# The last block's row maxima: two single products a step behind the scores of the same heads, in three banks

## The chip, the cores and the metric

The kernel runs on one core of one Trainium2 chip. The metric is device time in microseconds (us), the median of several runs. In the traces PE is TensorE's matmul side and PEld its weight loads, DVE is VectorE, ACT ScalarE, POOL GpSimd, and SP the engine whose queue issues most of the transfers. L262 means line 262 of the kernel before.

## The reference

Two layers run over a graph of N = 3327 nodes with 128 features, each followed by a residual sum and a layer norm. `adj` is a dense 0/1 matrix with ones on its diagonal.

```python
# layer 0
cos = beta[0] * (x @ x.T) / (norm2 @ norm2.T + 1e-07)
P = softmax(cos + (1.0 - adj) * -1e9, axis=1)
x = layernorm(x + P @ x)
# layer 1: d = 128 features, h = 8 heads
q = (x @ Wq.T).reshape(d, n, h)         # k and v alike
a = einsum('dnh,dmh->dnm', q, k) * d ** -0.5
a = softmax(a + adj + adj, axis=2)      # 128 matrices of 3327 x 3327
out = einsum('dnm,dmh->dnh', a, v)
x = layernorm(x + out.reshape(n, h * d) @ Wo.T)
```

Layer 1 is 128 independent attentions ("heads" below), each over 3327 queries and 3327 keys, with a contraction over only 8 numbers. The `reshape` is a plain one, so the heads are cut from the flat row order. Nearly all the time is spent there.

## The kernel before

**Precision.** Queries and keys are split into a high and a low part, so that a contraction over 8 becomes one over 4 x 8 = 32 rows of PE's array. Four heads fill the array's 128 rows, one in each row group of 32, and products of different row groups can be under way at the same time.

**Units and steps.** The 26 tiles of 128 queries are cut into nine blocks: eight of 384 queries and a last one of 256. The heads are cut into 32 groups of four. A unit is one block with one group; there are 288, block by block, and each has 26 steps, one for every tile of 128 keys: 7488 steps. The last block's 32 units are the final 832.

**One step** (loop at L873) makes the exponentials of one key tile for four heads, and multiplies the values by those of two steps ago:

- PE writes for two heads (`hs_b`) the shift, minus the row's maximum, into the two banks of `eb` (`shifts`, L788, matmul on L791) and adds the scores (`scores`, L797).
- ACT takes both through one exponential into `pb` (L898). POOL multiplies by `eT`, the exponential of twice the adjacency (L899).
- PE does the same for the other two heads (`hs_a`) in two banks `ea`, and adds the adjacency there by a product (`add_adj`, L778). ACT takes each bank through an exponential into `pa` (L922). The pool of `ea` has two buffers and a step uses both; `eb` has one of two banks.
- PE multiplies the values by the `pa` and `pb` of two steps ago (`weigh`, L808, `LAG = 2`).

Shifts, scores and search products use row groups of 32; adjacency and values use all 128 rows and groups of columns.

**The search.** The shift needs every row's maximum over all keys, so each score is computed twice: once with queries as output rows for the maximum, 33 steps ahead (`k = s + T + AHEAD`), and once with keys as output rows for the exponential. A search product is 128 queries by 512 keys of one head (L262). A "pair" is two heads' products in the two banks of tile `m2`, reduced by one VectorE instruction (L277); a "single" is one head's product in the one bank `m1`, with a reduction of its own (L298). The rest of the key range, chunk 6 with 256 keys, is done for two query tiles at once (L288, L302). `max_steps` (L231) lists a pair and a single for each of the 52 steps of two units. In a 384-query block each step has one of each. In the last block, two query tiles, a step needs two heads' products on average: even steps have a pair (heads 2, 3) and a single (head 0), odd steps a single (head 1) alone.

**Place in a step.** What is listed in `first` goes between the shifts and the scores of `hs_b`, `late` between the shifts and the scores of `hs_a`. For a 384-query block's search, the pair is first and the single late. For the last block's search, the single is first and the pair late, `hs_b` is always (2, 3) and `hs_a` (0, 1).

**Order.** The order on PE, ACT, DVE and POOL is the order in which the program is written (`manual_schedule`); the framework adds the semaphore waits from the tiles that are read and written. SP's transfers are issued in order too: a unit's keys, queries and values are loaded from step 2 of two units before. After a unit's search is complete, `shift_parts` (L313) makes its shifts ready with one VectorE and four POOL instructions, and in the unit before its own, `shift_turn` (L761) turns them at steps 22 and 23 of a 256-query unit into free columns of `ea`, from where ACT copies them (L916).

Of the kernel before, what the change touches and what calls it, by code (L numbers as in the profile page):

```python
# [10 lines left out]
F32 = mybir.dt.float32  # L11
# [8 lines left out]
P = 128  # L20
# [25 lines left out]
def gnn_two_layers(  # L46
# [116 lines left out]
    QB = QT * P  # L163
# [8 lines left out]
    units = [(b, g) for b in range(NB) for g in range(G4)]  # L172
# [4 lines left out]
    def width(b):  # L177
        return min(QT, T - b * QT) * P
# [46 lines left out]
    class Banks:  # L225
        pair = single = None
# [4 lines left out]
    def max_steps(u, w):  # L231

        if width(units[u][0]) == 2 * P:
            full = [((q,), c) for q in range(2) for c in range(6)] + [((0, 1), 6)]
            pairs = [x for v in (u, w) for k in full for x in ((v, (2, 3), *k), None)]
            ones = [(v, (a,), *k) for v in (u, w) for k in full for a in range(2)]  # L240
            return list(zip(pairs, ones))
        full = [((q,), c) for q in range(3) for c in range(6)]
        left = ((0, 1), 6)

        def one(v, hs, ks):
            return [(v, (a,), *k) for k in ks for a in hs]

        lo, hi = (0, 1), (2, 3)
        pairs = [(u, lo, *k) for k in full[:12]] + [(u, hi, *k) for k in full[:13]]
        pairs += [(u, hi, (2,), 6), (u, lo, (2,), 6)]  # L250
        last = one(w, hi, full[12:] + [left])
        ones = one(u, hi, full[13:] + [left]) + one(u, lo, full[12:] + [left]) + last[:1]
        pairs += [(w, hi, *k) for k in full[:12]]
        pairs += [(w, lo, *k) for k in full[:13]]
        ones += one(w, lo, full[13:] + [left]) + last[1:]
        assert len(pairs) == len(ones) == 2 * T
        assert not any(set(p[1]) & set(x[1]) for p, x in zip(pairs, ones))
        return list(zip(pairs, ones))
# [50 lines left out]
    def search(step):  # L309
        if step is not None:  # L310
            (max_pair if len(step[1]) == 2 else max_single)(*step)
# [32 lines left out]
    with ExitStack() as l0:  # L344
# [222 lines left out]
        with tc.manual_schedule(  # L567
# [9 lines left out]
            w = (T - 1) * P  # L577
# [7 lines left out]
            ones = const.tile([P, P], F32, name="ones")  # L585
# [30 lines left out]
            for c in range(NCH):  # L616
                tp, a, b = turn(ps_tp, lambda t: xn[:, t, :], c)
# [90 lines left out]
    with ExitStack() as at:  # L708
# [3 lines left out]
        ps_m = at.enter_context(tc.tile_pool(name="at_m", bufs=1, space=PSUM))  # L712
# [118 lines left out]
        with tc.manual_schedule(  # L831
            engines={
                mybir.EngineType.PE,
                mybir.EngineType.Activation,
                mybir.EngineType.DVE,
                mybir.EngineType.Pool,
            }
        ):
            for j in range(T):
                load_adj_tile(0, j)  # L840
            for i in range(2):
                load_values(us[i])
            us[0].kx = own.tile([P, NP], F32R, name="kx", bufs=2)
            nc.gpsimd.tensor_copy(
                us[0].kx.rearrange("p (t k) -> p t k", t=T),
                us[0].km.bitcast(F32).rearrange("p (k t) -> p t k", t=T),
            )
            keep_keys(us[0])
            for k in range(k_first, T + AHEAD):
                first_max(k)  # L850
            for j in range(T):
                exp_adj_tile(0, j)

            pp = at.enter_context(tc.tile_pool(name="at_p", bufs=4))
            ps_a = at.enter_context(tc.tile_pool(name="at_a", bufs=2, space=PSUM))
            ps_b = at.enter_context(tc.tile_pool(name="at_b", bufs=1, space=PSUM))
            ps_o = at.enter_context(tc.tile_pool(name="at_o", bufs=1, space=PSUM))
            acc = ps_o.tile([P, 512], F32, name="acc")
            nc.vector.memset(acc, 0.0)
            one = fix.tile([P, P], BF16, name="one")  # L860
            nc.vector.tensor_copy(one, ones)

            def new_a():
                return [ps_a.tile([P, 512], F32, name="ea") for _ in range(2)]

            e = ps_b.tile([P, 2, 512], F32, name="eb")
            for q in range(QT):
                shift_turn(us[0], q, e[:, 0, q * P : (q + 1) * P], True)
            nc.scalar.copy(us[0].cx, e[:, 0, :QB])  # L869

            todo = []
            turn = []
            for s in range(NU * T + LAG):  # L873
                i, j = divmod(s, T)
                u = us.get(i)
                if u is not None:
                    if j == 2 and i + 2 < NU:
                        load_keys(new_unit(i + 2))
                        load_queries(us[i + 2], own.tile([P, QB], F32R, name="qx"))
                        load_values(us[i + 2])  # L880
                    if j == 12 and i + 4 < G4:
                        gather(i + 4)
                    k = s + T + AHEAD
                    pair, single = max_step(k) or (None, None)

                    full = pair is not None and width(units[pair[0]][0]) == QB
                    first = pair if full else single
                    late = single if full else pair
                    hs_a = pair[1] if full else (0, 1)
                    hs_b = tuple(h for h in range(4) if h not in hs_a)  # L890

                    e_b = ps_b.tile([P, 2, 512], F32, name="eb")
                    b01 = [e_b[:, x] for x in range(2)]
                    shifts(u, b01, hs_b)
                    search(first)
                    scores(u, j, b01, hs_b, True)
                    pt_b = pp.tile([P, 2, QB], F32, name="pb")
                    nc.scalar.activation(pt_b[:, :, : u.nq], e_b[:, :, : u.nq], AF.Exp)  # L898
                    nc.gpsimd.tensor_tensor(  # L899
                        pt_b[:, :, : u.nq],  # L900
                        pt_b[:, :, : u.nq],
                        eT[:, j, : u.nq].unsqueeze(1).to_broadcast([P, 2, u.nq]),
                        ALU.mult,
                    )
                    e_a = new_a()
                    shifts(u, e_a, hs_a)
                    search(late)
                    scores(u, j, e_a, hs_a, False)
                    free = e_a[0][:, QB:]
                    x = us.get(i + 1)  # L910
                    copies = []
                    q = j - (T - 4)
                    if x is not None and 0 <= q < x.nt:
                        shift_turn(x, q, free, False)
                        copies.append(
                            lambda: nc.scalar.copy(x.cx[:, q * P : (q + 1) * P], free)  # L916
                        )
                    pt_a = pp.tile([P, 2, QB], F32, name="pa")
                    for h, e in enumerate(e_a):
                        add_adj(e, u, j)  # L920
                    for h, e in enumerate(e_a):
                        nc.scalar.activation(pt_a[:, h, : u.nq], e[:, : u.nq], AF.Exp)  # L922
                    for f in copies:
                        f()
                    if x is not None and not x.b:
                        order_keys(x, j)
                        if j == T - 1:
                            keep_keys(x)
                    pts = {}
                    for x in range(2):  # L930
                        pts[hs_a[x]], pts[hs_b[x]] = pt_a[:, x], pt_b[:, x]
                    todo.append((u, j, pts))

                    if k % (2 * T) in (T, 2 * T - 1):
                        v = us.get(k // (2 * T) * 2 + (k % (2 * T) > T))
                        if v is not None:
                            shift_parts(v)
                if s >= LAG:
                    w = todo.pop(0)
                    weigh(*w)  # L940
                    if w[1] == T - 1:
                        take(us.pop(w[0].i))

                if turn and turn[0][0] <= s:
                    exp_adj_tile(*turn.pop(0)[1:])
                if u is not None and i + 1 < NU and units[i + 1][0] != u.b:
                    load_adj_tile(u.b + 1, j)
                    turn.append((s + 5, u.b + 1, j))


    with ExitStack() as fi:
# [49 lines left out]
        w = (T - 1) * P  # L1001
# [43 lines left out]
```

## Time and profile before

The median of three runs is 15358.9 us (15358.85 to 15360.56).

| | |
|---|---|
| profiled execution | 15361.32 us, span 15359.5 us |
| mean granted TensorE clock | 0.995 |
| PE busy | 15192.6 us, 99% |
| DVE, POOL, ACT busy | 13818.7 (90%), 13765.0 (90%), 12755.2 us (83%) |
| DMA | 66 GB/s on average |
| search products (L262) | 23128 of 512 columns, 6804.0 us on PE, 471 ns each |
| pair reductions (L277) | 6753, 1225 ns each |
| single reductions (L298) | 6371, 681 ns each |

The busy time of one engine overlaps that of the others. Matmuls are pipelined, and their ends are modelled, so rows of PE overlap each other as well: the sum of their durations is far more than the span. The means of the groups above mix the blocks of 384 and of 256 queries. The last block's search runs from about 13923 us, while the eighth block's last steps are still under way, to about 15211 us.

### The profile page before, as it was taken

The page shows a single profiled execution, that of the slowest core. Times are in us where ns is not written, and L with a number is a line of the kernel's source. Part 1 is how long each engine was busy: PE and PEld are TensorE (multiplying, and loading weights), DVE is VectorE, ACT ScalarE, POOL GpSimd, SP SyncE. Part 2 cuts the span into 40 slices and gives each one's busy share as a digit, 9 for nine tenths or more (in the row PEclk, how much of TensorE's full clock was granted, in tenths as well). Part 3 has the DMA queues.
Part 4 walks back from the last instruction along what each step waited for, and adds up shares of the span by engine and source line. Part 5 has one row for each costly group of instructions (what it writes and reads, how often), then busy time and mean ns, then how long its engine had stood idle before and what let it go on. Part 6 is the DMA issues. An engine that isn't in the chain of part 4 may idle for free.

```text
span 15359.5 us, 494776 instructions
## 1 busy us (share of the span) xinstructions
PE 15192.6 (99%) x210460; PEld 6695.5 (44%) x210460; DVE 13818.7 (90%) x15851; ACT 12755.2 (83%) x25413; POOL 13765.0 (90%) x8979
## 2 busy tenths in 40 slices
PE   8899999999999999999999999999999999999999
PEld 5534444444444444444444444444444444444555
DVE  7889999999999999999999999999999999998776
ACT  7689998888888888888888888888888888888777
POOL 3389999999999999999999999999999999998887
PEclk9999999999999999999999999999999999999999
DMA  7732221111111111111111111111111111111112
GB/s 229 226 103 97 101 98 60 48 51 48 56 50 47 52 53 53 46 53 46 60 47 53 47 58 48 51 48 55 51 46 53 46 59 46 53 46 62 62 59 83
DMA packets 553135, 1018.81 MB, mean 66 GB/s; under 512 B 148711, under 2 KB 493284, under 8 KB 504582
## 3 DMA queue, kind: packets, MB, share of 16 engines
q1 hardware_dynamic: 547126, 965.00, 19.1%
q0 software_dynamic: 3792, 22.15, 0.8%
q8 instruction: 1648, 27.00, 0.7%
q14 instruction: 569, 4.66, 0.1%
HBM read 871.04 MB, written 192.54 MB: 69 GB/s over the span
## 4 chain that ended last, share of the span: by engine, by line
PE 96%; DMA 1%; DVE 1%; ACT 1%; issue 0%; SPq 0%; POOL 0%; DVEq 0%; ACTq 0%; POOLq 0%
PE acc L808 30%; PE ea L778 22%; PE m L262 16%; PE eb L791 13%; PE ea L791 10%; PE ea L797 1%; PE ea L764 1%; DMA aT_s<-aT 1%; PE eb L797 1%; PE acc L482 0%; PE pq L533 0%; PE sc L359 0%; ACT aT L397 0%; PE pp L993 0%; DMA qn_s<-high 0%
## 5 line engine op out<-in xcount | busy, mean ns | idle before, releaser
L899 POOL TENSOR_TENSOR pb<-pb,eT 128x768 f32<-128x768 f32 (+1 forms) x7488 | 13175.3, 1767 | 980.4 <-ACT pb L898 594.0
L277 DVE TENSOR_REDUCE mx<-m 128x2 f32<-128x1024 f32 x6753 | 8275.0, 1225 | 958.6 <-PE eb L797 555.4
L898 ACT ACTIVATE pb<-eb 128x768 f32<-128x768 f32 (+1 forms) x7488 | 5898.0, 788 | 2255.7 <-PE eb L797 1731.1
L262 PE MATMUL m<-kn,qx 32*128 32x512 f32 (+1 forms) x23128 | 6804.0, 471 | 0.1
L922 ACT ACTIVATE pa<-ea 128x384 f32<-128x384 f32 (+1 forms) x14976 | 6338.9, 478 | 23.0 <-PE ea L778 8.4
L808 PE MATMUL acc<-pb,vt 128*9 128x384 f32 (+1 forms) x29952 | 5903.7, 474 | 0.1
L808 PE MATMUL acc<-pa,vt 128*9 128x384 f32 (+1 forms) x29952 | 5903.7, 474 | 0.0
L298 DVE TENSOR_REDUCE mx<-m 128x1 f32<-128x512 f32 x6371 | 4338.5, 681 | 252.0 <-PE m L262 232.3
L791 PEld LDWEIGHTS <-one 3*128 3x128 bf16 x29952 | 1465.8, 91 | 5659.0 <-issue 4661.4
L778 PE MATMUL ea<-aT,two 128*32 128x384 bf16 (+1 forms) x59904 | 3715.6, 325 | 0.0
L797 PE MATMUL eb<-qx,kn 32*128 32x384 f32 (+1 forms) x13312 | 3030.2, 451 | 0.0
L797 PE MATMUL ea<-qx,kn 32*128 32x384 f32 (+1 forms) x13312 | 2938.7, 433 | 0.0
L262 PEld LDWEIGHTS m<-kn,qx 32*128 32x128 f32 x23128 | 2797.6, 182 | 216.3 <-DVE mx L298 4.7
L791 PE MATMUL ea<-cx,one 3*128 3x384 bf16 (+1 forms) x14976 | 2724.4, 324 | 0.2
L791 PE MATMUL eb<-cx,one 3*128 3x384 bf16 (+1 forms) x14976 | 2466.1, 326 | 16.9 <-ACT cx L869 16.7
L808 PEld LDWEIGHTS acc<-pa,vt 128*9 128x9 f32 x29952 | 1418.2, 91 | 399.9
L808 PEld LDWEIGHTS acc<-pb,vt 128*9 128x9 f32 x29952 | 1418.6, 91 | 387.0 <-issue 0.7
L778 PEld LDWEIGHTS <-two 128*32 128x32 bf16 x59904 | 938.1, 94 | 1421.5 <-issue 1231.0
L797 PEld LDWEIGHTS eb<-qx,kn 32*128 32x128 f32 x13312 | 1275.0, 188 | 0.0
L797 PEld LDWEIGHTS ea<-qx,kn 32*128 32x128 f32 x13312 | 1237.0, 182 | 8.0 <-issue 1.3
L302 DVE TENSOR_REDUCE mx<-m 128x2 f32<-128x512 f32 x1084 | 739.7, 682 | 20.3 <-PE m L262 19.1
L554 POOL CAST high<-row 128x512 fp32r<-128x512 f32 x104 | 96.0, 923 | 328.7 <-DMA qn_s<-high 209.9
(134 smaller groups left out, 5972.2 us busy)
## 6 DMA issues: line engine op xcount, KB each, us to landing
kn<-kp_s SPq DMA_DIRECT2D x512, 832.0 KB
vt<-v_s SPq DMA_DIRECT2D x288, 409.5 KB
kn<-kq_s SPq DMA_DIRECT2D x64, 832.0 KB
qx<-qp_s SPq DMA_DIRECT2D x1016, 48.0 KB
kn<-in_adj_dram SPq DMA_DIRECT2D x25, 1663.5 KB
qp_s<-qn_s SPq DMA_DIRECT2D x64, 416.0 KB
kp_s<-kx SPq DMA_DIRECT2D x32, 832.0 KB
kq_s<-kn_s SPq DMA_DIRECT2D x64, 415.9 KB
```

Source lines behind the costliest of these rows:

```text
L262: nc.tensor.matmul(dst, u.qx[rows(a), q * P : (q + 1) * P], u.km[rows(a), k0:k1], start=True, stop=True,)
L277: nc.vector.tensor_reduce(u.mx[:, h, qs[0], c], m, axis=AX.X, op=ALU.max)
L298: nc.vector.tensor_reduce(u.mx[:, a, qs[0], c : c + 1], m, axis=AX.X, op=ALU.max)
L302: nc.vector.tensor_reduce(u.mx[:, a, qs[0] : qs[1] + 1, c], m.rearrange("p (q k) -> p q k", q=2), axis=AX.X, op=ALU.max,)
L764: nc.tensor.matmul(dst[r], parts[u.i % 2][:, q, h], unit, start=start, stop=True, tile_position=(0, 32 * h), skip_group_check=True,)
L778: nc.tensor.matmul(e[r, : u.nq], two[:, r], aT[:, j, : u.nq], start=False, stop=True, tile_position=(0, 32 * c), skip_group_check=True,)
L791: nc.tensor.matmul(e[:, : u.nq], one[r], u.cx[r, : u.nq], start=True, stop=False, skip_group_check=True)
L797: nc.tensor.matmul(e[:, : u.nq], u.kx[rows(a), j * P : (j + 1) * P], u.qx[rows(a), : u.nq], start=False, stop=stop, skip_group_check=True,)
L808: nc.tensor.matmul(acc[32 * h : 32 * h + H + 1, : u.nq], u.vt[:, h, j], pts[h][:, : u.nq], start=(j == 0), stop=(j == T - 1), tile_positio ...
L898: nc.scalar.activation(pt_b[:, :, : u.nq], e_b[:, :, : u.nq], AF.Exp)
L899: nc.gpsimd.tensor_tensor(pt_b[:, :, : u.nq], pt_b[:, :, : u.nq], eT[:, j, : u.nq].unsqueeze(1).to_broadcast([P, 2, u.nq]), ALU.mult,)
L922: nc.scalar.activation(pt_a[:, h, : u.nq], e[:, : u.nq], AF.Exp)
```

## The change

Only the steps whose search is the last block's are touched.

- `max_steps` gives, for each step of the last block's search, two singles of two different heads in place of a pair and a single, or a single alone: heads 2 and 3 on even steps, 0 and 1 on odd steps. The number of products is the same.
- `hs_b`, the heads whose scores come first in a step, are those of the step's two singles; so they alternate from step to step.
- Both singles are issued behind the scores of `hs_b`, ahead of the shifts of `hs_a`.
- The banks of `m2` and `m1` are taken once, at the first such step, as three separate banks, and singles use them by turns.

```diff
         if width(units[u][0]) == 2 * P:
             full = [((q,), c) for q in range(2) for c in range(6)] + [((0, 1), 6)]
-            pairs = [x for v in (u, w) for k in full for x in ((v, (2, 3), *k), None)]
-            ones = [(v, (a,), *k) for v in (u, w) for k in full for a in range(2)]
-            return list(zip(pairs, ones))
+            return [
+                tuple((v, (a,), *k) for a in hs)
+                for v in (u, w)
+                for k in full
+                for hs in ((2, 3), (0, 1))
+            ]
...
-                    full = pair is not None and width(units[pair[0]][0]) == QB
-                    first = pair if full else single
-                    late = single if full else pair
-                    hs_a = pair[1] if full else (0, 1)
-                    hs_b = tuple(h for h in range(4) if h not in hs_a)
+                    behind = pair is not None and len(pair[1]) == 1
+                    if behind and not thirds:
+                        two_banks = ps_m.tile([P, 2, 512], F32, name="m2")
+                        thirds.extend(
+                            (two_banks[:, 0], two_banks[:, 1], ps_m.tile([P, 512], F32, name="m1"))
+                        )
+                        Banks.single = lambda: thirds.append(thirds.pop(0)) or thirds[-1]
+                    if behind:
+                        hs_b = pair[1] + single[1]
+                    else:
+                        hs_b = (2, 3) if pair is None else tuple(
+                            h for h in range(4) if h not in pair[1]
+                        )
+                    hs_a = tuple(h for h in range(4) if h not in hs_b)
...
                     shifts(u, b01, hs_b)
-                    search(first)
+                    if not behind:
+                        search(pair)
                     scores(u, j, b01, hs_b, True)
+                    if behind:
+                        search(pair)
+                        search(single)
...
                     shifts(u, e_a, hs_a)
-                    search(late)
+                    if not behind:
+                        search(single)
                     scores(u, j, e_a, hs_a, False)
```

More of the change, by code (lines that the diff above doesn't have):

```diff
@@ L869, in gnn_two_layers @@
             nc.scalar.copy(us[0].cx, e[:, 0, :QB])
+            thirds = []
             todo = []
```

## The prediction

> **What bounds the kernel now.** I read the page first, for its busy shares and the chain of waits.
>
> ```profile
> PE 15192.6 (99%) x210460; PEld 6695.5 (44%) x210460; DVE 13818.7 (90%) x15851; ACT 12755.2 (83%) x25413; POOL 13765.0 (90%) x8979
> ...
> PE 96%; DMA 1%; DVE 1%; ACT 1%; issue 0%; SPq 0%; POOL 0%; DVEq 0%; ACTq 0%; POOLq 0%
> ```
>
> This says "TensorE, everywhere". But a PE row runs from its issue to its modelled end, so a matmul that is issued and then stands behind another counts as busy: the page cannot show a PE that waits a little in every step. So I cut out the stretches that the change touches, by windows. They are 799 steps of 256 queries with the last block's search; then one unit (26 steps) of the kernel's tail, where the search is over; and 33 steps of 384 queries, which begin the last block's search. The columns are: window, length, busy time of PE, PEld, DVE, ACT and POOL, granted clock, DMA share, GB/s.
>
> ```profile
> 13986.16:15211.24 1225.08, 1224.83 (x21141) 622.47 (x21138) 972.22 (x1229) 977.54 (x2495) 1038.89 (x920) 1.00 0.18 60
> 15218.72:15256.34 37.62, 37.61 (x629) 18.74 (x626) 0.00 (x0) 31.97 (x81) 32.95 (x27) 1.00 0.02 4
> 13922.59:13986.16 63.57, 63.44 (x888) 26.02 (x885) 42.33 (x53) 59.05 (x126) 61.33 (x42) 1.00 0.24 65
> ```
>
> With the search a step takes 1225.08 / 799 = 1.533 us, without it 37.62 / 26 = 1.447. All the search products together cost 0.086 a step; the tail, still "100% PE", is no faster than that. Something other than the columns sets its pace. Next, the timeline of two steps with search (start, length, engine, line).
>
> ```profile
> 14600.82 0.66 ACT L922 ACTIVATE pa<-ea 128x256 f32<-128x256 f32 x2
> 14601.13 0.28 PE L791 MATMUL eb<-cx,one 3*128 3x256 bf16 x2
> 14601.53 0.38 PE L797 MATMUL ea<-qx,kn 32*128 32x256 f32 x2
> 14601.95 0.40 PE L778 MATMUL ea<-aT,two 128*32 128x256 bf16 x8
> 14602.36 0.66 ACT L922 ACTIVATE pa<-ea 128x256 f32<-128x256 f32 x2
> 14602.72 0.28 PE L791 MATMUL eb<-cx,one 3*128 3x256 bf16 x2
> 14603.07 0.39 PE L797 MATMUL ea<-qx,kn 32*128 32x256 f32 x2
> 14603.35 0.60 ACT L898 ACTIVATE pb<-eb 128x512 f32<-128x512 f32 x1 [0.34 <-PE m L262]
> 14603.39 0.40 PE L778 MATMUL ea<-aT,two 128*32 128x256 bf16 x8
> 14603.85 0.66 ACT L922 ACTIVATE pa<-ea 128x256 f32<-128x256 f32 x2
> ```
>
> The first step (14601.13) holds a pair and a single, the second (14602.72) a single alone. The two `pa` exponentials end at 14601.48 and 14603.02; the `ea` scores are issued at 14601.53 and 14603.07, each 0.05 later, directly behind the second `ea` shift. That shift needs the bank that the second `pa` has just read: `ea` has two banks, and a step uses both. So a loop closes once a step: second `ea` shift, scores, the adjacency (L778), two exponentials, next shift. Its legs: 0.42 + 0.41 + 0.66 + 0.05 = 1.54 in the step with the pair (the pair's products stand between shift and scores), 0.32 + 0.46 + 0.66 + 0.05 = 1.49 in the other: 3.03 together, the distance from 14601.13 to 14604.16, where the third step starts. The tail shows the bare loop:
>
> ```profile
> 15228.81 0.66 ACT L922 ACTIVATE pa<-ea 128x256 f32<-128x256 f32 x2
> 15229.17 0.28 PE L791 MATMUL eb<-cx,one 3*128 3x256 bf16 x2
> 15229.52 0.38 PE L797 MATMUL ea<-qx,kn 32*128 32x256 f32 x2
> 15229.67 0.60 ACT L898 ACTIVATE pb<-eb 128x512 f32<-128x512 f32 x1 [0.20 <-PE eb L797]
> 15229.83 0.40 PE L778 MATMUL ea<-aT,two 128*32 128x256 bf16 x8
> 15230.24 0.66 ACT L922 ACTIVATE pa<-ea 128x256 f32<-128x256 f32 x2
> ```
>
> Again 0.05 behind the exponentials (15229.47 to 15229.52), then 0.31 + 0.41 + 0.66 + 0.05 = 1.43. This loop, not PE's columns, sets the last block's step.
>
> **The change part by part.**
>
> *The pair leaves the place between second shift and scores.* That leg falls from 0.42 to 0.32, its length where the search product is elsewhere: 0.10 per two steps.
>
> *The single leaves the place ahead of the `eb` scores.* `pb` then starts 0.50 after the step's start, as in the tail (15229.17 to 15229.67), not 0.63 (14602.72 to 14603.35). At 0.63 its 0.60 held up `pa` in the single-only steps (leg 0.46 against 0.41): 0.05 more per two steps. So 3.03 becomes about 2.88.
>
> *Two singles arrive behind the `eb` scores, in the scores' own row groups.* One row group there has shift, score, search product in series. Shifts of 384 columns take 332 ns (row between 10000 and 12000 us) and 278 here for 256, so 0.42 ns a column: 0.11 for 256, 0.21 for 512, and 0.17 until a product is complete. A score is issued at 0.04 and takes 0.36, so it streams from 0.12 to 0.23. When may the third weights be loaded? No step of before shows three in a row group with the third unhindered. The nearest row is a step whose single is two products of 256 columns in one row group:
>
> ```profile
> 14331.29 0.38 PE L262 MATMUL m<-kn,qx 32*128 32x256 f32 x1
> 14331.39 0.18 PEld L262 LDWEIGHTS m<-kn,qx 32*128 32x128 f32 x1
> 14331.51 0.28 PE L262 MATMUL m<-kn,qx 32*128 32x256 f32 x1
> ```
>
> The second load starts 0.10 into the first product, as its stream begins, and the second product follows without a gap. Then the third load here goes from 0.12, the product streams from 0.23 to 0.45, and with 0.10 to drain (a pair's load to L778 is 0.42 = 0.11 load, 0.21 stream, 0.10) L778 could start at 0.55. The loop puts it at 0.35 + 0.31 = 0.66. So I cost both products at nothing, covered with 0.11 to spare. The bounds: a load held until the score's stream ends gives 0.23 + 0.42 = 0.65, still covered; one held until the score is complete at 0.40 gives 0.82, not covered. I take the first, by that row; the last is a rival.
>
> [...]
>
> *The banks.* PE gets two waits on VectorE a step. Each product waits for the reduction three before it; the second one's is the first reduction of the step before. Product complete at 0.62, reduction from 0.67, 0.686 long (its row over these 799 steps): done at 1.35, seen 0.05 later at 1.40, needed at 1.43 + 0.12 = 1.55. Margin 0.15. Behind that wait all of PE stands, the shifts first, so without the margin it would cost its excess in every step.
>
> *VectorE* goes from 2 x 0.686 + 1.216 = 2.59 per two steps to 4 x 0.686 = 2.74, under the new 2.88 even without the 0.09 by which neighbours overlap. *GpSimd's* multiply is 1.274 a step, and the four small operations per unit (0.9 together) delay one multiply, whose result PE wants two steps later, with 1.3 to spare. *PE* issues as many products and loads as before (four searches per two steps). *SP's queue* is not moved past: the loads of a unit are over some 12 us into it, and used about 28 us in.
>
> *The 33 steps at 384 queries* take 63.57 / 33 = 1.93. GpSimd's multiply of 1.83 (its row between 10000 and 12000 us) is the lower bound (-3 us in all), the 1.97 of the 23 steps just before (45.41 us) the upper (+1.5); those of the 33 with a single alone take 1.88, so I take -1.5.
>
> **Sum.** A unit like the tail's, plus half of the 0.01 by which a leg with a search elsewhere is longer: 37.62 + 0.1 = 37.72, or 1.451 a step; 799 x 1.451 = 1159.2, which is 65.9 under 1225.1. With -1.5: -67.4. The profiled execution took 15361.3 (span 15359.5), so 15293.9; it is 2.4 above the median 15358.9, against which I forecast 15291.5, 0.44% faster.
>
> **The rivals.**
>
> *PE is the bound after all* (the chain of waits' 96%): the columns are the same, so 15359. For it: PE has no idle time. Against: the tail, with 1024 columns a step fewer, keeps to the exponentials' ends.
>
> *Partly covered*: the third load later than 0.23, up to 0.30. Then L778 at 0.66 to 0.72, up to 0.06 a step or 48 us lost: up to 15339.
>
> *Slower: the third load waits until the score is complete* (0.40). L778 at 0.82, 0.77 from there to the next step, 0.017 for the unit's slow steps: 1.607, +0.074 x 799 = +59, or 15418. It decides from a load later than 0.32, where the step is back at 1.533. Against it: the load at 14331.39.
>
> *The two banks cut from one tile are waited for as one.* Then one step in three waits for the second reduction of the step before (0.67 + 2 x 0.60 = 1.87 to 1.95, seen at 0.56 of this step), and L778 comes at 0.56 + 0.42 = 0.98, 0.32 late: +0.11 a step on 1.451, +0.025 against now, about +20: 15379. Nothing in the trace shows such a tile.
>
> **How the numbers follow.** Forecast 0.78, partly covered 0.06, PE the bound 0.06, banks as one 0.04, late load 0.06. A measurement here can tell about 0.2%, 31 us. Faster: the forecast and the partly covered, 0.84; same: PE and banks, 0.10; slower: 0.06. The forecast's own range: at best every step as in the tail, -69, with -3: 15287; some us below for the 0.06 that `pb`'s earlier start may add. At worst 0.02 a step beyond the loop and +1.5: 15311. With most of the partly covered (its worst is 15339), 15283 to 15330 leaves about 2 in 10 out.
>
> **What would show it.** Right: steps of about 1.435 alternating no more; `ea` shifts still 0.05 behind `pa`'s ends; `pb` 0.50 after the step's start; search products issued at about 0.23, L778 at 0.66; reductions of 0.69 with idle time left. Wrong: L778 at 0.7 or later with the shifts off `pa`'s ends (row groups bound it), or PE waiting on L298 (banks).

## The result

The changed kernel takes 15889.4 us (median of 4 runs, 15851.9 to 15901.9), against 15359.6 before: 1.0342 times as long, 95% interval 1.033 to 1.0355, 530 us slower. The forecast was 15291.5, in 15283 to 15330. It failed by its size and by its sign.

First the page of the kernel after: its span, busy shares and chain of waits.

```profile
span 15895.7 us, 495194 instructions
...
PE 15490.3 (97%) x210460; PEld 6774.4 (43%) x210460; DVE 13905.1 (87%) x16267; ACT 12790.5 (80%) x25413; POOL 13765.4 (87%) x8979
...
PE 93%; DVE 3%; DMA 1%; ACT 1%; issue 1%; SPq 0%; POOL 0%; DVEq 0%; POOLq 0%; ACTq 0%
```

VectorE stands in the chain with 3% in place of 1%, and PE is busy for 97% of the span in place of 99%. The time is in the stretches that the change touches. By windows of the same 799 steps and the same 33 (length, busy time of PE, PEld, DVE, ACT, POOL, then granted clock, DMA share, GB/s):

```profile
13994.40:15746.09 1751.69, 1523.29 (x21143) 707.47 (x21140) 1059.52 (x1630) 1013.95 (x2496) 1040.82 (x921) 0.82 0.13 42
13919.05:13994.40 75.35, 66.73 (x886) 28.73 (x883) 44.05 (x69) 59.90 (x126) 61.33 (x42) 1.00 0.20 55
```

The 799 steps take 1751.7 in place of 1225.1 (+526.6), the 33 take 75.4 in place of 63.6 (+11.8): 538.4, against 536.3 between the two profiled executions. Nothing else moved by more than a few us. Two things are new: PE is idle for 228 of the 1752 us, where it had been idle for 0.3, and the granted clock is 0.82 in place of 1.00. What PE waits for, by two rows of the waits view of that stretch (total us, times, longest):

```profile
...
PEld m L265 <- DVE mx L301: 313.6, 356, 1.3
...
PE m L265 <- DVE mx L301: 209.9, 340, 1.0
```

The loads of the search products (L265, before L262) wait for the single's reduction (L301, before L298). Three steps in a row, where the clock was full, show which loads and which reductions:

```profile
14618.97 0.28 PE L794 MATMUL eb<-cx,one 3*128 3x256 bf16 x2
14619.09 0.19 PEld L265 LDWEIGHTS m<-kn,qx 32*128 32x128 f32 x1
14619.64 0.69 DVE L301 TENSOR_REDUCE mx<-m 128x1 f32<-128x512 f32 x1 [0.32 <-PE m L265]
14620.38 0.18 PEld L265 LDWEIGHTS m<-kn,qx 32*128 32x128 f32 x1 [1.10 <-DVE mx L301]
14620.38 0.50 PE L265 MATMUL m<-kn,qx 32*128 32x512 f32 x1 [0.78 <-DVE mx L301]
14620.81 0.40 PE L781 MATMUL ea<-aT,two 128*32 128x256 bf16 x8
14621.57 0.28 PE L794 MATMUL eb<-cx,one 3*128 3x256 bf16 x2
14621.70 0.19 PEld L265 LDWEIGHTS m<-kn,qx 32*128 32x128 f32 x2
14622.24 0.40 PE L781 MATMUL ea<-aT,two 128*32 128x256 bf16 x8
14622.24 1.29 DVE L301 TENSOR_REDUCE mx<-m 128x1 f32<-128x512 f32 x2 [0.64 <-PE m L265]
14623.00 0.28 PE L794 MATMUL eb<-cx,one 3*128 3x256 bf16 x2
14623.59 0.18 PEld L265 LDWEIGHTS m<-kn,qx 32*128 32x128 f32 x2 [0.38 <-DVE mx L301]
```

Steps begin at 14618.97, 14621.57 and 14623.00. In the first, one product is loaded 0.12 in, its reduction runs from 14619.64 to 14620.33, and only 0.05 after that the second product is loaded, at 14620.38. It waited for a reduction of its *own* step. With three banks by turns these two products use the two halves of `two_banks`: the second writes a bank that this reduction does not read. In the second step (bank of `m1`, then the first half) both products are loaded 0.13 in, and the step takes 1.43, just as forecast: L781 at 0.67. In the third (second half, then `m1`) both stand behind a load that waits until 14623.59, 0.06 after the previous step's second reduction, the one of the *other* half, has ended (14622.24 + 1.29 = 14623.53). Where the clock is full the medians of the three kinds are 2.61, 1.43 and 1.77.

So the theory after the result, A: the framework orders accesses to `two_banks` by tile and not by bank. Its rival, B: two products behind the scores, in their row groups, or two reductions a step, cost this by themselves. A ratio below is to the median of before on the same chip, with its 95% interval. That median is 15364.86 for two runs, the one with products in the gap and the one with both singles ahead of the scores, and 15359.25 for the other four.

### The profile page after: what moved, and what is told of

It reads as the page before. It is cut to its first block, busy times and chain, and to the rows that moved or that the text cites. A ratio compares the mean times of both kernels' runs of the same rounds, so it can differ in the third digit from the quotient of the medians.

```text
span 15895.7 us, 495194 instructions
## 1 busy us (share of the span) xinstructions
PE 15490.3 (97%) x210460; PEld 6774.4 (43%) x210460; DVE 13905.1 (87%) x16267; ACT 12790.5 (80%) x25413; POOL 13765.4 (87%) x8979
## 4 chain that ended last, share of the span: by engine, by line
PE 93%; DVE 3%; DMA 1%; ACT 1%; issue 1%; SPq 0%; POOL 0%; DVEq 0%; POOLq 0%; ACTq 0%
PE acc L811 30%; PE ea L781 21%; PE m L265 17%; PE eb L794 12%; PE ea L794 8%; DVE mx L301 2%; PE ea L800 1%; PE eb L800 1%; PE ea L767 1%; DMA aT_s<-aT 1%; PE acc L485 0%; PE pq L536 0%; PE sc L362 0%; DMA qn_s<-high 0%; PE pp L1011 0%
## 5 line engine op out<-in xcount | busy, mean ns | idle before, releaser
L280 DVE TENSOR_REDUCE mx<-m 128x2 f32<-128x1024 f32 x6369 | 7806.7, 1226 | 959.8 <-PE eb L800 563.4
L265 PE MATMUL m<-kn,qx 32*128 32x512 f32 (+1 forms) x23128 | 6762.5, 470 | 237.0 <-DVE mx L301 217.7
L811 PE MATMUL acc<-pb,vt 128*9 128x384 f32 (+1 forms) x29952 | 6034.9, 484 | 0.1
L811 PE MATMUL acc<-pa,vt 128*9 128x384 f32 (+1 forms) x29952 | 6034.5, 484 | 0.0
L301 DVE TENSOR_REDUCE mx<-m 128x1 f32<-128x512 f32 x7139 | 4823.0, 682 | 667.3 <-PE m L265 658.7
L794 PEld LDWEIGHTS <-one 3*128 3x128 bf16 x29952 | 1416.0, 91 | 5674.4 <-issue 4774.7
L781 PE MATMUL ea<-aT,two 128*32 128x384 bf16 (+1 forms) x59904 | 3780.7, 330 | 0.0
L800 PE MATMUL eb<-qx,kn 32*128 32x384 f32 (+1 forms) x13312 | 3065.2, 456 | 0.0
L265 PEld LDWEIGHTS m<-kn,qx 32*128 32x128 f32 x23128 | 2804.1, 184 | 561.5 <-DVE mx L301 330.5
L794 PE MATMUL ea<-cx,one 3*128 3x384 bf16 (+1 forms) x14976 | 2669.9, 328 | 0.2
L781 PEld LDWEIGHTS <-two 128*32 128x32 bf16 x59904 | 943.1, 95 | 1475.2 <-issue 1313.1
L305 DVE TENSOR_REDUCE mx<-m 128x2 f32<-128x512 f32 x1148 | 780.0, 683 | 53.7 <-PE m L265 53.2
```

What stands on the lines that cost most here:

```text
L265: nc.tensor.matmul(dst, u.qx[rows(a), q * P : (q + 1) * P], u.km[rows(a), k0:k1], start=True, stop=True,)
L280: nc.vector.tensor_reduce(u.mx[:, h, qs[0], c], m, axis=AX.X, op=ALU.max)
L301: nc.vector.tensor_reduce(u.mx[:, a, qs[0], c : c + 1], m, axis=AX.X, op=ALU.max)
L305: nc.vector.tensor_reduce(u.mx[:, a, qs[0] : qs[1] + 1, c], m.rearrange("p (q k) -> p q k", q=2), axis=AX.X, op=ALU.max,)
L781: nc.tensor.matmul(e[r, : u.nq], two[:, r], aT[:, j, : u.nq], start=False, stop=True, tile_position=(0, 32 * c), skip_group_check=True,)
L794: nc.tensor.matmul(e[:, : u.nq], one[r], u.cx[r, : u.nq], start=True, stop=False, skip_group_check=True)
```

## Experiments

### Three tiles of one bank each

The pool of the banks is closed where the last block's search begins, and another with three tiles takes its place.

```diff
-        ps_m = at.enter_context(tc.tile_pool(name="at_m", bufs=1, space=PSUM))
+        own_m = ExitStack()
+        ps_m = own_m.enter_context(tc.tile_pool(name="at_m", bufs=1, space=PSUM, side="right"))
...
-                        two_banks = ps_m.tile([P, 2, 512], F32, name="m2")
-                        thirds.extend(
-                            (two_banks[:, 0], two_banks[:, 1], ps_m.tile([P, 512], F32, name="m1"))
-                        )
+                        own_m.close()
+                        ps_t = at.enter_context(tc.tile_pool(name="at_t", bufs=1, space=PSUM, side="right"))
+                        thirds.extend(ps_t.tile([P, 512], F32, name=f"t{x}") for x in range(3))
```

> The kernel after, with one edit: the three banks are three tiles of one bank each, from a pool opened where the last block's search begins, in place of two halves of one tile and a tile. Theory A (one tile): after is slow because the framework orders accesses by tile and not by bank, so a product into one half of the two-bank tile waits for the reduction of the other half, although that reads another bank. Then no product waits here, every step is like the one in three of after that takes 1.43 us, and the time is the forecast's 15291 (15283 to 15311). Rival B (place): two products behind the scores in the same row groups, or two reductions a step, cost the time by themselves; whose tile a bank belongs to changes nothing, and the time stays at 15850 to 15900.

Measured: 15294.1, ratio 0.9957 (0.9945 to 0.997): 65 us faster than before, 595 faster than after, with the same instructions in the same places. The windows of its 799 and 33 steps, and its timeline:

```profile
13984.47:15143.70 1159.23, 1159.15 (x21142) 670.60 (x21138) 1033.29 (x1629) 998.81 (x2496) 1037.77 (x920) 1.00 0.19 64
13921.81:13984.47 62.66, 62.66 (x886) 28.40 (x882) 43.03 (x69) 58.70 (x126) 60.98 (x42) 1.00 0.24 66
```

```profile
14600.84 0.66 ACT L940 ACTIVATE pa<-ea 128x256 f32<-128x256 f32 x2
14601.20 0.28 PE L795 MATMUL eb<-cx,one 3*128 3x256 bf16 x2
14601.24 0.36 PE L801 MATMUL eb<-qx,kn 32*128 32x256 f32 x2
14601.27 0.27 PE L795 MATMUL ea<-cx,one 3*128 3x256 bf16 x1
14601.33 0.19 PEld L265 LDWEIGHTS t<-kn,qx 32*128 32x128 f32 x2
14601.44 0.40 PE L265 MATMUL t<-kn,qx 32*128 32x512 f32 x2
14601.55 0.38 PE L801 MATMUL ea<-qx,kn 32*128 32x256 f32 x2
14601.70 0.60 ACT L915 ACTIVATE pb<-eb 128x512 f32<-128x512 f32 x1 [0.21 <-PE eb L801]
14601.86 0.12 PEld L782 LDWEIGHTS <-two 128*32 128x32 bf16 x8
```

A holds and B falls. The clock is back at 1.00, and this is the step that the prediction described: third load 0.13 after the step's start, product at 0.24, exponential of `eb` at 0.50, `ea` scores 0.05 behind the end of `pa` (14601.50), adjacency at 0.66. The 799 steps take 1.4509 each; the prediction's sum had 1.451. This is the fastest of all the kernels here.

### The two products first, then the two reductions

`max_single` is made a generator that stops between its product and its reduction: `next` issues the product, `list` the reduction.

```diff
                     if behind:
-                        search(pair)
-                        search(single)
+                        both = [max_single(*x) for x in (pair, single)]
+                        for x in both:
+                            next(x)
+                        for x in both:
+                            list(x)
```

> The kernel after with its two-bank tile kept, but the two products of a step are issued first and then their two reductions, in place of product, reduction, product, reduction. Theory A (one tile): in the step that uses both halves the second product no longer has a reduction of the same tile ahead of it, so the wait of about 1.3 us in every third step goes; what is left is one step in three that waits for the second reduction of the step before, about 0.32 us: 15375 to 15390, with the clock near that of before. Rival B (place): the same products and reductions are in the same places on PE and VectorE, so 15850 to 15900.

Measured: 15385.9, ratio 1.0017 (1.0008 to 1.0026). The shared tile is still there, and yet 504 of the 530 us are gone. What is left is one step in three:

```profile
14611.61 0.28 PE L799 MATMUL eb<-cx,one 3*128 3x256 bf16 x2
14611.73 0.19 PEld L265 LDWEIGHTS m<-kn,qx 32*128 32x128 f32 x1
14612.20 0.18 PEld L265 LDWEIGHTS m<-kn,qx 32*128 32x128 f32 x1 [0.28 <-DVE mx L302]
14612.63 0.40 PE L786 MATMUL ea<-aT,two 128*32 128x256 bf16 x8
14613.40 0.28 PE L799 MATMUL eb<-cx,one 3*128 3x256 bf16 x2
14613.62 0.18 PEld L265 LDWEIGHTS m<-kn,qx 32*128 32x128 f32 x2
```

The second product of such a step is loaded 0.59 after its start, behind the second reduction of the step before, and the step takes 1.78; the two other kinds take 1.43 (medians). This is what the prediction's rival of the shared tile had priced (0.56, and 15379). In the step after it both loads come 0.22 after its start and not 0.12, as they would if its first product waits for the reduction of the other half too; that costs nothing. The run shows where that rival went wrong: it was worked out for this order of the program, and the change has the other one.

### The half clock: products in the gap

`third` counts the steps with the last block's search, from 0; the steps with `third % 3 == 0` are those that use both halves. In them `e_a` is taken earlier than otherwise.

```diff
                         search(pair)
+                        if third % 3 == 0:
+                            e_a = new_a()
+                            for _ in range(6):
+                                nc.tensor.matmul(
+                                    e_a[1][:, : u.nq],
+                                    two,
+                                    aT[:, j, : u.nq],
...
                         search(single)
...
-                    e_a = new_a()
+                    if not behind or third % 3:
+                        e_a = new_a()
+                    if behind:
+                        third += 1
```

> The kernel after with its waits, and six products of 128 rows and 256 columns that nothing reads, put on PE in the long wait of every third step, between the first single and the second (they go into a bank of ea that the shift overwrites). Theory (the gaps halve the clock): after loses time twice, by waiting, and by a clock that is granted by half for 619 of the 1752 us because PE stands still for some 0.8 us in every third step. With the gap filled the clock stays full, the waits are as long as before, and the steps take the 2.61, 1.43 and 1.77 that after's steps take where the clock is full: 1.935 x 799 = 1546, 321 over before, 15680 (15640 to 15700). If the half clock has another cause, 15850 to 15900, or more by what the products themselves take.

Measured: 15704.1, ratio 1.0222 (1.0208 to 1.0235), 185 us less than after, although PE does 1600 products more. Its 799 steps:

```profile
14000.25:15552.69 1552.44, 1502.00 (x22744) 788.94 (x22741) 1059.45 (x1629) 1012.91 (x2495) 1041.72 (x920) 1.00 0.14 48
```

The clock is 1.00, and the medians of the three kinds of step are 2.61, 1.43 and 1.78, the waits of after to 0.01. So of the 526.6 us over before the clock is 1751.7 - 1552.4 = 199, and the waits, less what the change gains without them, are 1552.4 - 1225.1 = 327. Against the three-tile kernel, which has no such waits, they are 1552.4 - 1159.2 = 393. The time is 4 us outside what was expected: the 33 steps at 384 queries took 77.9, 14 more than before (12 more in after), and the expectation had counted none of that.

### The parts of the change alone, on the kernel before

The pair behind the scores of its heads, everything else as before (`full` is false in the last block's search):

```diff
                     scores(u, j, b01, hs_b, True)
+                    if not full:
+                        search(late)
...
-                    search(late)
+                    if full:
+                        search(late)
                     scores(u, j, e_a, hs_a, False)
```

> The kernel before with one part of the change alone: in the last block's search the pair goes behind the scores of its own heads (2, 3), ahead of the other heads' shifts; pair and single, their tiles and the single's place are as before. Loop theory: the leg between second shift and adjacency falls from 0.42 to 0.32 in every second step, 0.10 x 400 = 40 us: 15319. PE-bound rival (the same columns take the same time): 15359. Late-load rival (the third weights of a row group wait until the score is complete, adjacency at 0.82 of the step, where it is now): 15359 too, but with the shifts no longer 0.05 behind the exponentials.

Measured: 15346.8, ratio 0.9991 (0.9983 to 1.0): 12 us, where the loop theory had 40. In its profile the 799 steps take 1210.3 us, 15 less than before.

The single behind the scores, the pair late as before:

```diff
-                    search(first)
+                    if full:
+                        search(first)
                     scores(u, j, b01, hs_b, True)
+                    if not full:
+                        search(first)
```

> The kernel before with the other part alone: in the last block's search the single goes behind the scores of hs_b, in place of ahead of them; the pair stays late. Loop theory: the exponential of eb starts at 0.50 in place of 0.63 and no longer holds up the next one in the single-only steps, 0.05 x 400 = 20 us: 15339. PE-bound rival: 15359. If the single, now issued later on the row group that the shifts need next, delays them by its stream of 0.21, the steps get up to 0.2 longer every other step: 15359 to 15440.

Measured: 15350.7, ratio 0.9994 (0.9985 to 1.0003): 9 us, where the theory had 20. The interval includes no change; in the profile the 799 steps take 1213.6 us, 11 less than before. The two terms of the prediction's sum do not add up part by part: alone they are worth 21 together, and with the two singles in three banks 65. A step with pair and single of the first kernel shows what takes most of its gain back:

```profile
14614.24 0.68 DVE L298 TENSOR_REDUCE mx<-m 128x1 f32<-128x512 f32 x1
14614.54 0.65 ACT L925 ACTIVATE pa<-ea 128x256 f32<-128x256 f32 x2
14614.89 0.28 PE L791 MATMUL eb<-cx,one 3*128 3x256 bf16 x2
14614.98 0.18 PEld L262 LDWEIGHTS m<-kn,qx 32*128 32x128 f32 x1
14615.33 0.28 PE L791 MATMUL ea<-cx,one 3*128 3x256 bf16 x1
14615.62 0.60 ACT L900 ACTIVATE pb<-eb 128x512 f32<-128x512 f32 x1 [0.43 <-PE m L262]
14615.65 0.40 PE L778 MATMUL ea<-aT,two 128*32 128x256 bf16 x8
14616.11 0.65 ACT L925 ACTIVATE pa<-ea 128x256 f32<-128x256 f32 x2
```

The pair's leg is indeed short, 0.32 from the second shift (14615.33) to the adjacency. But the single is loaded 0.09 late, 0.06 behind the end of the reduction of the single before it (14614.92), and the second shift comes 0.14 behind the end of `pa` (14615.19) in place of 0.05; the median over these steps is 0.12. That is 0.07 of the 0.10. The exponential of `eb` starts 0.73 into the step, and now it is this step whose `pa` is held up (leg 0.46), while in the odd steps the leg fell to 0.42 (median). The change has a third part, three banks by turns: with them the trace of the three-tile kernel has no load of a search product that waits for a reduction. In the second kernel:

```profile
14615.09 0.28 PE L791 MATMUL eb<-cx,one 3*128 3x256 bf16 x2
14615.44 0.18 PEld L262 LDWEIGHTS m<-kn,qx 32*128 32x128 f32 x2
14615.59 0.60 ACT L901 ACTIVATE pb<-eb 128x512 f32<-128x512 f32 x1 [0.21 <-PE m L262]
14615.87 0.40 PE L778 MATMUL ea<-aT,two 128*32 128x256 bf16 x8
14616.27 0.66 ACT L925 ACTIVATE pa<-ea 128x256 f32<-128x256 f32 x2
```

The exponential of `eb` is early (0.50) and `pa` is free of it (leg 0.40), as the theory had it. The late pair is loaded at 0.35, and the adjacency starts 0.43 behind its load; the loop still runs through the pair's products. Why the gain is 9 or 11 us and not 20 is not shown.

### Both singles ahead of the scores, in three tiles

```diff
-                        hs_b = pair[1] + single[1]
+                        hs_a = pair[1] + single[1]
...
-                    if not behind:
-                        search(pair)
+                    search(pair)
+                    if behind:
+                        search(single)
                     scores(u, j, b01, hs_b, True)
-                    if behind:
-                        search(pair)
-                        search(single)
```

> The three-tile kernel with one part undone: the two singles of a step stand ahead of the scores of hs_b, in the row groups of the other two heads (which are then hs_a), as the single did before, in place of behind the scores of their own heads. Loop theory with the legs of the prediction: every step becomes like the single-only step of before, the exponential of eb starting at 0.63 in place of 0.50 and holding up the next one, 0.32 + 0.46 + 0.66 + 0.05 = 1.49 a step in place of 1.43, so about 0.05 x 799 = 40 us more than the three-tile kernel: 15335. If the place in the step does not matter once no product waits for a reduction, 15294 as with three tiles.

Measured: 15333.7, ratio 0.998 (0.9971 to 0.9989), where 15335 was expected. Two steps of it:

```profile
14601.47 0.28 PE L795 MATMUL eb<-cx,one 3*128 3x256 bf16 x2
14601.82 0.31 PE L795 MATMUL ea<-cx,one 3*128 3x256 bf16 x2
14602.14 0.60 ACT L911 ACTIVATE pb<-eb 128x512 f32<-128x512 f32 x1 [0.33 <-PE t L265]
14602.18 0.40 PE L782 MATMUL ea<-aT,two 128*32 128x256 bf16 x8
14602.64 0.65 ACT L936 ACTIVATE pa<-ea 128x256 f32<-128x256 f32 x2
14602.94 0.28 PE L795 MATMUL eb<-cx,one 3*128 3x256 bf16 x2
```

The exponential of `eb` starts 0.67 into the step and `pa` 0.46 behind the adjacency, not 0.41. So the place behind the scores is worth some 35 us (the ratios to before, 0.998 and 0.9957, differ by 0.0023), by the exponential that it lets start early.

## Why the prediction was wrong

**The step that failed** is the one headed "The banks", in its sentence "Each product waits for the reduction three before it". That is which bank is used again, not what is waited for. From it came the margin of 0.15 and a cost of nothing. The trace of after has the second product of every third step waiting for the reduction that is one before it, with PE idle for 0.78 us. The three-tile kernel, whose trace has no such wait, took 15294.1.

**The rival that named the cause was mis-sized.** "The two banks cut from one tile are waited for as one" was given 0.04 and +20 us; it is the mechanism, and it cost 595 us against the three-tile kernel, 530 against before. It was priced as if both products of a step stood ahead of both reductions. The code has product, reduction, product, reduction, so with one tile the first reduction stands between the products of its own step. The wait is then a full product and reduction: the load comes 1.41 into the step in place of 0.12, and the step takes 2.61 in place of 1.43; the rival had 0.32 more in a third of the steps. With the order that it assumed, 15385.9 was measured against its 15379. Its chance was also too low: "nothing in the trace shows such a tile" bounds nothing, and a term that no row bounds should not have been given a margin.

**A term was missing**: 199 us are a clock that the prediction took as constant (1.00 before, 0.82 in after). It was the second effect of the same waits, and nothing in the prediction asked what an idle PE would do to it.

**What held.** The loop through the two banks of `ea` sets the step: 0.05 between the end of `pa` and the `ea` scores, in before, in after's undisturbed steps and in the three-tile kernel. There the third load of a row group overlaps the product ahead of it (load at 0.13, while the score runs from 0.04 to 0.40), as the load at 14331.39 did in the kernel before (the product ahead of it runs from 14331.29 to 14331.67). VectorE, GpSimd and the transfers carried the faster step (busy for 1033.3 and 1037.8 of its 1159.2 us, DMA share 0.19). The sum was right for the kernel without the shared tile: 1.451 a step against 1.4509, 15291.5 against 15294.1.

**What held only as a whole.** The sum's two terms, 0.10 and 0.05 per two steps, were read as if each could be had alone (-40 and -20). Alone they gave -12 and -9. With the pair moved alone, the wait for the single's reduction and the held-up `pa` stood right behind it; for the single alone the missing part stays open.

"PE is the bound after all" is refuted by the three-tile kernel: the same columns take 66 us less in those 799 steps. The late load and the partly covered case are refuted by its third load at 0.13.

## What to carry to other kernels

When buffers by turns are cut from one allocation, find out whether the framework orders them as one, and write the waits down in program order, with every reader that stands between two writers; one tile a bank made 595 us of difference here without moving an instruction. PE with a gap of 0.78 us in every third step lost more than the gap here (199 us more, at a clock of 0.82): look at the granted clock in the window before adding up waits. And a leg that is shortened alone shows what stands next behind it; where several constraints end close to each other, the parts of a change need not add up: here 12 and 9 us alone, 65 together.

## What was unexpected of the hardware

The clock was granted by half (0.50) in 619 of after's 1752 us, although PE never waited longer than 1.0 us at a stretch and was idle only 13% of the time. In the same kernel with products in those gaps (idle for 50 of 1552 us) it was 1.00, and it was 1.00 in the kernel whose loads waited 0.3 us per third step (PE idle for 1.2 of 1249 us). A product row shows it: the two search products of a good step take 0.40 together, and at half clock

```profile
14617.37 0.62 PE L265 MATMUL m<-kn,qx 32*128 32x512 f32 x2
```

The trace of after shows more. All 267 changes of its clock in the 799 steps lie on a grid of 3.413 us. Of the stretches of this grid at full clock, none of the 100 with less than 0.77 us of idle PE was followed by half clock, and all 25 with more than 0.86 were; of the 199 between, most with one whole gap of 0.78, 108 were. The 33 steps at 384 queries have a gap of 0.78 in every second stretch and kept 1.00. So idle time alone does not decide there, and what else does is not shown.

A product that stands later in the program started earlier. In the three-tile kernel the first `ea` shift (14601.27), in another row group than the `eb` scores (14601.24 to 14601.60), starts ahead of the search products (14601.44) that precede it in the program.
